# A decoder layer on one core: who issues the DMAs, in which order, and how often weights are loaded

## The chip, the cores and the metric

The kernel runs on one core of a Trainium2 chip. The core has a matrix engine (TensorE, PE in the profile; its weight loads are PEld), a vector engine (VectorE, DVE), an activation engine (ScalarE, ACT), a general engine (GpSimd, POOL) and SyncE (SP), which in this kernel issues DMAs. Every engine runs its own list of instructions in the order in which it was built and waits on semaphores. The metric is the time of one launch on the device in microseconds, lower is better.

## The reference, cut to what matters

Sixteen independent sequences of 256 positions and width 512 go through one layer of three parts, each followed by a residual sum and a layernorm (cut; biases and masks shortened):

```python
# 1: state-space mixer, 1024 channels (d), 16 states (n)
hs, gate = W_in_states @ x, W_in_gates @ x
hs   = silu(causal_conv4(hs))
dt   = softplus(W_dtproj @ (W_dt @ hs) + b)        # [d, l]
Bm, Cm = W_b @ hs, W_c @ hs                          # [n, l]
s    = exp(A * dt) * s + dt * Bm * hs                # scan over l, for each d, n
y    = (sum_n s * Cm + D * hs) * silu(gate)
x    = layernorm(x + W_out @ y)
# 2: cross attention, 16 heads of 16; x is read as [256 channels, 512 positions]
q, k, v = Wq @ x, Wk @ ctx, Wv @ ctx
x    = layernorm(x + softmax(mask * (q.k / 4) ...) @ v)
# 3: feed-forward, ternary weights, 8-bit activations
h    = silu(a) * b   with  a, b = quant(x) @ quant(w_gate_up)
x    = layernorm(x + quant(h) @ quant(w_down))
```

## The kernel before

Each batch (sequence) passes through stages that are cut into small closures ("thunks"). The table `WIN` gives each stage a window in time measured in batches: `P` and `R` (`prep`: input projection with convolution; time step, B and C, softplus), `M` (the scan, 34 thunks), `T` and `U` (gate and output projection of the two channel halves), `K`, `L` (keys, first layernorm, queries), `A` (values and attention, 10 steps of 4 parts), `N` (normalising the attention), `F` (feed-forward) and `W` (quantising weights, once). `place` spreads a stage's thunks over its window, and all thunks are called in the order of these times. So up to four batches are in work at once. The order of the calls is only a priority: the tile framework schedules the instructions itself, each engine's list included, with SyncE's list of DMAs among them, and puts in the semaphore waits.

Tiles come from pools by tag, each tag with a fixed number of buffers; a new tile waits until the oldest buffer of its tag is free. The parts that the change touches:

- **Weights.** `wload` (line 91) loads a tile with tag `wout`, 3 buffers, from SyncE's queue at the place of use. `project` (line 260) loads a `win` tile and uses it at once; `outproj` (line 502) loads four `wout` tiles for each of two row tiles `lt`, so each twice; `up` and `down` (lines 667 and 707) load the 8-bit tiles `fw` for each of two row tiles `t`.
- **Softplus** (line 321) makes dt and dt*u for eight channel tiles and stores them to a DRAM tile `dtd` (line 360). Its work tiles `e` and `l` share the tag `h` (8 buffers) with the scan.
- **Scan.** `fetch(d)` (line 373) reads `dtr` and `dur` back, replicated over the partitions, 512 KB each, one per channel tile. `unit(d, g)` (line 398) multiplies on POOL (line 403), makes four exps on ACT (line 409) and runs two scans on DVE (line 411). `tail`, two units later (`LAG`), multiplies by C on POOL (line 383); after four of them TensorE sums over the states (line 389).
- **Attention.** `split_store` (line 450) writes queries and keys as a high and a low part to `sq` and `sk` in DRAM (line 459). `fetch(g)` (line 519) reads two heads back into `qk` tiles (10 buffers). `step(i, c)` computes scores of head pair `i` for their maxima (lines 530 and 558) and, for pair `i - 2`, exps (line 564) and the products with the values (line 574). `maxima` (line 535) turns the maxima into two rows per head: it writes them to a DRAM tile `md` (line 547) and reads that into rows 62 to 65 of the query tile (line 548). The products go to `so` in DRAM (line 596). `norm` (line 603) reads sums and products back.

Every DMA of this kernel is issued by SyncE.

Of the kernel before, what the change touches and what calls it, by code (L numbers as in the profile page):

```python
# [13 lines left out]
ALU = mybir.AluOpType  # L14
# [22 lines left out]
WIN = {'P': (-1.15, -0.888), 'R': (-0.611, -0.455), 'M': (0.0, 0.8), 'T': (0.476, 0.576), 'U': (0.812, 0.912), 'L': (0.991, 1.041), 'K': (0.773, 0.826), 'A': (1.018, 1.938), 'N': (2.099, 2.147), 'F': (2.57, 3.237), 'W': (0.0, 1.0)}  # L37
# [5 lines left out]
HB = 8  # L43
PTB = 3
QKB = 10
F4B = 3
LAG = 2
# [4 lines left out]
def decoder_kernel(ctx, tc, x, xT, ctx_in, mask, winT, wdtT, wbcT, wdpT, woutT, dvec, wqkvT, bqk, bv, wguT, wdnT, out):  # L52
# [35 lines left out]
    def f4(shape, dt=F32):  # L88
        return ap_.tile(shape, dt, tag="f4", name=nm("f4"), bufs=F4B)

    def wload(src):
        w = mp.tile(list(src.shape), F32, tag="wout", name=nm("wout"), bufs=3)
        nc.sync.dma_start(out=w, in_=src)
        return w
# [21 lines left out]
    al = mt("h", [P, NDT, NB4, NS], HB)  # L116
# [36 lines left out]
    wq = const([P, 2, 256], F32, "wq")  # L153
# [3 lines left out]
    def setup_mask():  # L157
        nc.sync.dma_start(out=wq, in_=wqkvT[:, :, 0:256])
# [38 lines left out]
    def w_load(j):  # L197
        c, r = divmod(j, 2)
        src = wguT[:, 2 * r : 2 * r + 2, c * 512 : (c + 1) * 512] if c < 8 else wdnT[:, (c - 8) * 4 + 2 * r : (c - 8) * 4 + 2 * r + 2, :]
        w = mt("h", [P, 2, 512], HB)  # L200
        nc.sync.dma_start(out=w, in_=src)
        return w

    def setup_w():
# [4 lines left out]
        def total():  # L209
# [4 lines left out]
            ones = mt("h", [P, P], HB)  # L214
# [6 lines left out]
        def quant(j):  # L221
# [5 lines left out]
            q = at("fw", [P, 2, 512], 3, FP8)  # L227
# [32 lines left out]
    def project(ps_t, xt, c0):  # L260

        for i in range(2):
            w = mt("win", [P, 4, P], 3)
            nc.sync.dma_start(out=w, in_=winT[:, :, c0 + i * P : c0 + (i + 1) * P])
            for k in range(4):
                nc.tensor.matmul(ps_t[:, i, :], w[:, k, :], xt[:, k, :], start=k == 0, stop=k == 3)  # L266


    def prep(b):
        st = S[b]  # L270
        th = []

        def load():
            st["xT"] = xload(b)
            st["u"] = [None, None]

        def inproj(d0):
            hs = mm_ps([P, 2, L], "P")
            z = mt("tmp", [P, 2, L], 2)
            project(hs, st["xT"], d0 * P)  # L280
# [14 lines left out]
        def ts_bc():  # L295
            p = mm_ps([P, 512], "P")
            for d in range(NDT):
                if d % 4 == 0:
                    wdt = wload(wdtT[:, d : d + 4, :])
                nc.tensor.matmul(p[:, :L], wdt[:, d % 4, :], st["u"][d // 4][:, d % 4, :], start=d == 0, stop=d == NDT - 1)  # L300
            ts = mt("ts", [P, L], 1)
            nc.scalar.copy(ts, p[:, :L])
            st["ts"] = ts
            wbc = wload(wbcT)
            p2 = mm_ps([P, 512], "P")
            for d in range(NDT):
                nc.tensor.matmul(p2[:32, :L], wbc[:, d, :], st["u"][d // 4][:, d % 4, :], start=d == 0, stop=d == NDT - 1)
            bc = mt("tmp", [32, L], 2)
            nc.scalar.copy(bc, p2[:32, :L])
            bcd = dr.tile([32, L], F32, tag="bcd", name=nm("bcd"), bufs=2)  # L310
            nc.sync.dma_start(out=bcd, in_=bc)
            st["bcd"] = bcd
# [8 lines left out]
        def softplus():  # L321

            st["dtd"] = dr.tile([2, NDT, DB, NB4, L], F32, tag="dtd", name=nm("dtd"), bufs=3)
            xs, es, ls = [], [], []
            for hf in range(2):
                X = mt("dt", [P, 4, L], 2)
                xs.append(X)
                wdp = wload(wdpT[:, hf * 512 : (hf + 1) * 512])
                for i2 in range(2):
                    p = mm_ps([P, 2, L], "P")  # L330
                    for i in range(2):
                        c = (2 * i2 + i) * P
                        nc.tensor.matmul(p[:, i, :], wdp[:, c : c + P], st["ts"], start=True, stop=True)
                    for i in range(2):
                        d = hf * 4 + 2 * i2 + i
                        nc.scalar.activation(X[:, 2 * i2 + i, :], p[:, i, :], AF.Identity, bias=dv[:, d, 6:7])
                e = mt("h", [P, 4, L], HB)
                es.append(e)
                nc.scalar.activation(e, X, AF.Abs)
                nc.scalar.activation(e, e, AF.Exp, scale=-1.0)  # L340
            for hf in range(2):
                l = mt("h", [P, 4, L], HB)
                ls.append(l)
                nc.scalar.activation(l, es[hf], AF.Ln, bias=1.0)
            for hf in range(2):
                for i2 in range(2):
                    s = slice(2 * i2, 2 * i2 + 2)
                    X, e, l = xs[hf][:, s, :], es[hf][:, s, :], ls[hf][:, s, :]
                    t = mm_ps([P, 2, L], "P")
                    nc.scalar.activation(t, e, AF.Identity, bias=1.0)  # L350
                    nc.vector.scalar_tensor_tensor(t, t, 1.0, e, ALU.subtract, ALU.subtract)
                    nc.vector.scalar_tensor_tensor(t, X, 0.0, t, ALU.max, ALU.subtract)
                    nc.vector.tensor_tensor(t, t, l, ALU.add)
                    dtu = mt("dtu", [P, 2, L], 2)
                    nc.vector.tensor_tensor(dtu, t, st["u"][hf][:, s, :], ALU.mult)
                    nc.scalar.copy(X, t)  # L356
                    for k, src in ((0, X), (1, dtu)):
                        for i in range(2):
                            dst = st["dtd"][k, 4 * hf + 2 * i2 + i].rearrange("c g l -> g c l")
                            nc.sync.dma_start(out=dst, in_=src[:, i, :])  # L360

        th = [load] + [lambda d=d: inproj(d) for d in range(0, NDT, 2)]
        return {"P": th, "R": [ts_bc, bcast, softplus]}
# [3 lines left out]
    def scan(b):  # L367
        st = S[b]
        th = []
# [3 lines left out]
        def fetch(d):  # L373
            st["rep"] = []
            for k, tag in ((0, "dtr"), (1, "dur")):
                t = mt(tag, [P, NB4, L], 2)
                src = st["dtd"][k, d].rearrange("c g l -> c (g l)")
                nc.sync.dma_start(out=t, in_=src[None].broadcast_to([NB4, DB, NB4 * L]))
                st["rep"].append(t)
# [18 lines left out]
        def unit(d, g):  # L398
            if g == 0:
                fetch(d)  # L400
            dt, dtu = st["rep"]
            hh = mt("h", [P, NS // NB4, L], HB)
            nc.gpsimd.tensor_tensor(hh, st["B"], dtu[:, g, None, :].broadcast_to([P, NS // NB4, L]), ALU.mult)  # L403
            for h2 in range(2):
                t = dA_t[dA_i[0] % 2]
                dA_i[0] += 1
                for i in range(2):
                    j = 2 * h2 + i
                    nc.scalar.activation(t[:, i, 1:], dt[:, g, 1:], AF.Exp, scale=A[:, d, g, j : j + 1])  # L409
# [6 lines left out]
        for d in range(NDT):  # L416
            for g in range(NB4):
                th.append(lambda d=d, g=g: unit(d, g))
        th += [lambda: tail(pend.pop(0))] * LAG
        return th  # L420


    def attn(b):
        st = S[b]
        st["sq"], st["sk"] = sq_t[b % 2], sk_t[b % 2]
        th = []

        def load():
# [11 lines left out]
            mr = at("mr", [P, 64], 1)  # L440
            nc.sync.dma_start(out=mr, in_=mask[b, 0].rearrange("(a e) -> a e", a=8)[None].broadcast_to([16, 8, 64]))
            st["mr"] = mr
# [8 lines left out]
        def split_store(m, p, bcol, dst, slots_hi, slots_lo):  # L451
# [5 lines left out]
            for t, slots in ((hi, slots_hi), (lo, slots_lo)):  # L457
                for s in slots:
                    nc.sync.dma_start(
                        out=dst[m * 8 : m * 8 + 8, R0 + s * HD : R0 + (s + 1) * HD, :],  # L460
                        in_=t.bitcast(F32),
                    )

        def kproj():
            wk = wload(wqkvT[:, :, 256:512])
            for m in range(2):
                p = mm_ps([P, 512], "K")
                for k in range(2):
                    nc.tensor.matmul(p, wk[:, k, m * P : (m + 1) * P], st["ctx"][k], start=k == 0, stop=k == 1)
                split_store(m, p, 1, st["sk"], (0, 2), (1,))  # L470

        def vproj():
            wv = wload(wqkvT[:, :, 512:768])
            bvh = bv_t.rearrange("p (h d) -> p h d", h=NH)
            for s in range(0, 4, 2):
                p = mm_ps([P, 2, 256], "V")
                for i in range(2):
                    for k in range(2):
                        nc.tensor.matmul(p[:, i, :], st["ctx"][k][:, (s + i) * P : (s + i + 1) * P], wv[:, k, :], start=k == 0, stop=k == 1)
                for i in range(2):  # L480
                    v = vaug[:, s + i, :, 0:HD]
                    nc.vector.tensor_tensor(v, p[:, i, :].rearrange("p (h d) -> p h d", h=NH), bvh, ALU.add)
                    nc.scalar.mul(v, v, st["ms"][:, s + i : s + i + 1])

        def gate_load():
            st["xTg"] = xload(b)

        def gated(d0):
            g = mm_ps([P, 2, L], "G")
            project(g, st["xTg"], DI + d0 * P)  # L490
# [10 lines left out]

        def outproj(hf, lt):
            p = mm_ps([P, 512], "O")
            for i in range(4):
                w = wload(woutT[:, 4 * hf + i, :])
# [310 lines left out]
```

## Time and profile before

| | |
|---|---|
| median of 3 runs | 5132.09 us (5129.36 to 5134.6) |
| profiled execution | 5123.51 us |
| its span, first to last instruction | 5121.4 us |
| mean granted TensorE clock | 0.751 |
| busy: PE, DVE, POOL, ACT | 3462.3, 2966.0, 2544.8, 2421.9 us |
| DMA | 688.54 MB, mean 134 GB/s, 43.4% of 16 engines' time |
| first and last store of `out` | 1128.8 and 5117.1 us |

A profile is one execution. "Busy" is the time in which an engine has an instruction in work. The chain that ended last is followed back from the last instruction, at each step to what released it. A wait is named by the engine and line that waited and by what ended the wait. "SPq" is SyncE's instruction list itself, where DMAs are issued. The granted clock is the share of full clock that TensorE got.

### The profile page before, as it was taken

What the parts mean: (1) busy time and instruction counts of PE and PEld (TensorE: products, weight loads), DVE (VectorE), ACT (ScalarE), POOL (GpSimd) and SP (SyncE); (2) the same over time, 40 slices, a digit from 0 to 9 for tenths busy, and PEclk for the clock granted to TensorE, in tenths of its full rate; (3) what the DMA queues carried; (4) which work ended last, traced back from release to release, by engine and by line L of the source; (5) the groups of instructions that cost most, each with busy time, mean ns of one, the idle gap of its engine ahead of it and who ended that gap; (6) DMA issues with size and microseconds to landing.
All of it is one profiled execution on the core that took longest, in us unless ns stands there. A gap on an engine that the chain in (4) does not pass through costs nothing.

```text
span 5121.4 us, 50817 instructions
## 1 busy us (share of the span) xinstructions
PE 3462.3 (68%) x16386; PEld 1616.7 (32%) x16386; DVE 2966.0 (58%) x4254; ACT 2421.9 (47%) x4700; POOL 2544.8 (50%) x1367
## 2 busy tenths in 40 slices
PE   3234677867767777666768576686666768675876
PEld 2112333333323333322323223232332324332332
DVE  2566557565656666465556565465565655665543
ACT  2343446454454555435454454455445444544433
POOL 1645457465554555455445565355554544666100
PEclk7666676877777787777868778686776868777868
DMA  5455343544435453443534435344443534434233
GB/s 153 138 175 170 103 138 119 154 135 131 147 121 177 120 155 124 138 135 115 161 120 141 128 116 156 112 146 126 137 141 111 168 116 136 145 126 151 85 103 103
DMA packets 488723, 688.54 MB, mean 134 GB/s; under 512 B 53944, under 2 KB 266936, under 8 KB 488456
## 3 DMA queue, kind: packets, MB, share of 16 engines
q1 hardware_dynamic: 488456, 685.29, 43.4%
q8 instruction: 130, 2.13, 0.2%
q14 instruction: 137, 1.12, 0.1%
HBM read 569.15 MB, written 122.29 MB: 135 GB/s over the span
## 4 chain that ended last, share of the span: by engine, by line
PE 31%; DMA 27%; DVE 18%; ACT 9%; SPq 4%; issue 4%; POOL 1%; DVEq 0%; ACTq 0%; POOLq 0%
DVE h L411 9%; DMA wout<-in_woutT 8%; PE mm L266 6%; PE sc L530 6%; PE mm L389 4%; DVE mx L558 4%; PE mm L506 4%; DMA md<-mhl 3%; PE av L574 3%; DMA sq<-qf 3%; ACT pT L564 2%; DMA qk<-sk 2%; PE sc L718 2%; DMA fw<-dn_q 2%; ACT dA L409 2%
## 5 line engine op out<-in xcount | busy, mean ns | idle before, releaser
L403 POOL TENSOR_TENSOR h<-B,dur 128x1024 f32<-128x1024 f32 x512 | 1196.2, 2364 | 1272.4 <-PE mm L389 858.1
L383 POOL TENSOR_TENSOR h<-h,C 128x1024 f32<-128x1024 f32 x512 | 1199.3, 2363 | 371.0 <-DVE h L411 327.5
L409 ACT ACTIVATE dA<-dtr,A 128x255 f32<-128x255 f32 x2048 | 951.5, 473 | 855.7 <-DVE h L411 775.6
L530 PE MATMUL sc<-qk,qk 64*128 64x512 f32 x2048 | 926.9, 627 | 547.1 <-DMA qk<-sk 187.1
L411 DVE TENSOR_TENSOR_SCAN h<-dA,h 128x512 f32<-128x512 f32 x1024 | 1210.4, 1207 | 58.7 <-ACT dA L409 42.8
L558 DVE TENSOR_REDUCE mx<-sc 128x1 f32<-128x512 f32 x1024 | 673.5, 679 | 542.3 <-PE sc L530 539.2
L564 ACT ACTIVATE pT<-sc 128x512 f32<-128x512 f32 x1024 | 582.2, 592 | 773.4 <-PE sc L530 768.8
L530 PEld LDWEIGHTS sc<-qk,qk 64*128 64x128 f32 x2048 | 363.0, 232 | 1229.4 <-issue 626.5
L266 PE MATMUL mm<-xT,win 128*128 128x256 f32 x2048 | 559.2, 428 | 161.4 <-DMA win<-in_winT 69.0
L506 PE MATMUL mm<-wout,u 128*128 128x512 f32 x512 | 329.3, 752 | 418.2 <-DMA wout<-in_woutT 392.6
L266 PEld LDWEIGHTS mm<-xT,win 128*128 128x128 f32 x2048 | 426.9, 215 | 287.7 <-ACT dt L356 60.5
L574 PE MATMUL av<-pT,vaug 128*32 128x256 f32 x4096 | 436.4, 495 | 49.6 <-ACT pT L564 47.4
L389 PE MATMUL mm<-h,sel 128*32 128x256 f32 x4096 | 397.3, 472 | 94.6 <-POOL h L383 86.7
L286 DVE SCALAR_TENSOR_TENSOR tmp<-mm,cw,tmp 128x255 f32<-128x255 f32 (+2 forms) x384 | 182.7, 478 | 247.0 <-ACT tmp L283 240.7
L507 DVE TENSOR_TENSOR xres<-mm,xres 128x512 f32<-128x512 f32 x64 | 43.8, 686 | 401.0 <-PE mm L506 398.5
L506 PEld LDWEIGHTS mm<-wout,u 128*128 128x128 f32 x512 | 99.2, 225 | 515.4 <-DMA wout<-in_woutT 360.5
L389 PEld LDWEIGHTS mm<-h,sel 128*32 128x32 f32 x4096 | 151.9, 131 | 306.5 <-issue 170.3
L718 PE MATMUL sc<-fw,f 128*128 128x512 fp8e4 x512 | 137.4, 415 | 140.9 <-DMA fw<-dn_q 140.6
L245 POOL TENSOR_SCALAR lrs<-lmv 128x2 f32<-128x2 f32 x48 | 10.0, 218 | 392.0 <-DVE lmv L243 390.9
L621 POOL TENSOR_TENSOR qk<-qk,qk 128x512 f32<-128x512 f32 x32 | 40.6, 1269 | 329.1 <-DMA qk<-sr 126.5
L574 PEld LDWEIGHTS av<-pT,vaug 128*32 128x32 f32 x4096 | 97.7, 122 | 275.0 <-ACT pT L564 131.5
L678 PE MATMUL sc<-fw,xqT 128*128 128x512 fp8e4 x512 | 164.9, 454 | 23.3 <-DVE mx L558 13.4
(116 smaller groups left out, 3373.7 us busy)
## 6 DMA issues: line engine op xcount, KB each, us to landing
win<-in_winT SPq DMA_DIRECT2D x256, 256.0 KB
dtr<-dtd SPq DMA_DIRECT2D x128, 512.0 KB
dur<-dtd SPq DMA_DIRECT2D x128, 512.0 KB
wout<-in_woutT SPq DMA_DIRECT2D x256, 256.0 KB
fw<-gu_q SPq DMA_DIRECT2D x256, 256.0 KB
qk<-sq SPq DMA_DIRECT2D x128, 256.0 KB
qk<-sk SPq DMA_DIRECT2D x128, 256.0 KB
fw<-dn_q SPq DMA_DIRECT2D x128, 256.0 KB
```

The costliest lines, as they stand in the source:

```text
L266: nc.tensor.matmul(ps_t[:, i, :], w[:, k, :], xt[:, k, :], start=k == 0, stop=k == 3)
L383: done.append((hh, nc.gpsimd.tensor_tensor(hh, hh, st["C"], ALU.mult)))
L389: m = nc.tensor.matmul(red[DB * g : DB * g + DB, :L], sel, h[:, j, :], start=j == 0, stop=j == NS // NB4 - 1, tile_position=(0, DB * g))
L403: nc.gpsimd.tensor_tensor(hh, st["B"], dtu[:, g, None, :].broadcast_to([P, NS // NB4, L]), ALU.mult)
L409: nc.scalar.activation(t[:, i, 1:], dt[:, g, 1:], AF.Exp, scale=A[:, d, g, j : j + 1])
L411: nc.vector.tensor_tensor_scan(seg, t.rearrange("p n l -> p (n l)"), seg, 0.0, ALU.mult, ALU.add)
L506: nc.tensor.matmul(p, st["u"][hf][:, i, lt * P : (lt + 1) * P], w, start=i == 0, stop=i == 3)
L530: nc.tensor.matmul(p, lhs[rows, c * P : (c + 1) * P].bitcast(F32R), rhs[rows, :].bitcast(F32R), start=True, stop=True)
L558: nc.vector.tensor_reduce(st[("mx", i)][:, j, c : c + 1], p, AX.X, ALU.max)
L564: x = nc.scalar.activation(e[:, j, :], p, AF.Exp, scale=DSC)
L574: m = nc.tensor.matmul(av[32 * k : 32 * k + 32, :], vaug_f[:, c, c0 : c0 + 32], e[:, j, t * L : (t + 1) * L], start=c == 0, stop=c == 3, t ...
L718: nc.tensor.matmul(p, hT[:, 4 * q + i, :], w[:, i, :], start=q + i == 0, stop=q == 3 and i == 3)
```

## The change

All thunks now go into one heap with a time each (`at_time`), and a thunk can put a later one there (`defer`). SyncE's list is taken from the framework's scheduler: its DMAs stand in the order in which the thunks issue them. The other engines' lists are still scheduled. With it:

- every load has a thunk of its own, most of them `LEAD` = 0.08 of a batch ahead of the use; `wout` and `fw` tiles are loaded once and used for both row tiles, with four buffers each, and `win` has four; other weights have tag `wr`, 3 buffers;
- stores of `so`, of the high parts of queries and keys, of dt and of B and C are issued by ScalarE; stores that stay with SyncE are mostly deferred by 0.01 to 0.03;
- `maxima` writes its rows with four DMAs from SBUF to SBUF, without `md`;
- softplus is cut into its two halves, has work tiles `s` (3 buffers) of its own, and writes dt*u over `e`; `dtr` and `dur` are fetched in halves of 256 KB;
- `norm` is cut into four thunks, and the product of its reciprocal sums with the mask moves from DVE to POOL;
- buffers: `h` 7 instead of 8, `pT` 2 instead of 3, `qk` 8 instead of 10; `LAG` 1 instead of 2;
- the times of all stages are new; the scan takes the whole batch time instead of 0.8 of it.

The diff, cut to its core:

```diff
-HB = 8
-PTB = 3
-QKB = 10
-F4B = 3
-LAG = 2
+HB = 7
+PTB = 2
+QKB = 8
+LEAD = 0.08
+LAG = 1
...
+    heap = []
+    now = [0.0]
+    def at_time(t, f):
+        uid[0] += 1
+        heapq.heappush(heap, (t, uid[0], f))
+    def defer(dt, f):
+        at_time(now[0] + dt, f)
+    def wload(src, tag="wr", bufs=3, dt=F32):
+        w = mp.tile(list(src.shape), dt, tag=tag, name=nm(tag), bufs=bufs)
         nc.sync.dma_start(out=w, in_=src)
         return w
...
+    def win_load(c0):
+        return [wload(winT[:, :, c0 + i * P : c0 + (i + 1) * P], "win", 4) for i in range(2)]
...
+            nc.scalar.dma_start(out=st["bcd"], in_=bc)
...
+        def softplus(hf):
+            Xf = mt("s", [P, 4, L], 3)
+            ef = mt("s", [P, 4, L], 3)
...
+                nc.scalar.activation(X, e, AF.Ln, bias=1.0)
+                nc.vector.tensor_tensor(t, t, X, ALU.add)
+                nc.vector.tensor_tensor(e, t, st["u"][hf][:, s, :], ALU.mult)
+                nc.scalar.copy(X, t)
+                for i in range(2):
+                    nc.scalar.dma_start(out=dst(0, d + i), in_=X[:, i, :])
+            for d in range(4):
+                nc.sync.dma_start(out=dst(1, 4 * hf + d), in_=ef[:, d, :])
...
+        for t, f in (
+            (-0.5 - LEAD, ts_load), (-0.5, time_step), (-0.46 - LEAD, bc_load), (-0.46, bc), (-0.3, bcast),
+            (-0.38 - LEAD, lambda: dt_load(0)), (-0.38, lambda: softplus(0)),
+            (-0.26 - LEAD, lambda: dt_load(1)), (-0.26, lambda: softplus(1)),
+        ):
+            at_time(b + t, f)
...
-        def fetch(d):
+        def fetch(d, g):
             for k, tag in ((0, "dtr"), (1, "dur")):
+                t = mt(tag, [P, 2, L], 2)
+                src = st["dtd"][k, d, :, g : g + 2, :].rearrange("c g l -> c (g l)")
...
+                t = b + (4 * d + g + 0.5) / 32
+                if g % 2 == 0:
+                    at_time(t - 0.05, lambda d=d, g=g: fetch(d, g))
+                at_time(t, lambda d=d, g=g: unit(d, g))
...
+            store(nc.scalar, hi, slots_hi)
+            defer(0.01, lambda: store(nc.sync, lo, slots_lo))
...
+        def wout_load(hf):
+            st[("wout", hf)] = [wload(woutT[:, 4 * hf + i, :], "wout", 4) for i in range(4)]
         def outproj(hf, lt):
             for i in range(4):
-                w = wload(woutT[:, 4 * hf + i, :])
-                nc.tensor.matmul(p, st["u"][hf][:, i, lt * P : (lt + 1) * P], w, start=i == 0, stop=i == 3)
+                nc.tensor.matmul(p, st["u"][hf][:, i, lt * P : (lt + 1) * P], st[("wout", hf)][i], start=i == 0, stop=i == 3)
...
-            md = dr.tile([G, 2, 4, P], F32, tag="md", name=nm("md"), bufs=4)
-            for j in range(G):
-                nc.sync.dma_start(out=md[j].rearrange("q a t -> a q t"), in_=mhl[4 * j : 4 * j + 4].bitcast(F32))
-            nc.sync.dma_start(out=QS[KROWS - 2 : KROWS + 2], in_=md.rearrange("j q a t -> (j q) (a t)"))
+            def store():
+                for j in range(G):
+                    for q in range(2):
+                        r = KROWS - 2 + 2 * j + q
+                        nc.sync.dma_start(out=QS[r : r + 1, :], in_=mhl[4 * j : 4 * j + 4, q, :].bitcast(F32))
+            defer(0.03, store)
...
-                        nc.sync.dma_start(out=dst.rearrange("h r t -> (h r) t"), in_=o[64 * t : 64 * t + 64, :])
+                        nc.scalar.dma_start(out=dst.rearrange("h r t -> (h r) t"), in_=o[64 * t : 64 * t + 64, :])
...
-            nc.vector.tensor_tensor(rc, rc, st["mr"], ALU.mult)
+            nc.gpsimd.tensor_tensor(rc, rc, st["mr"], ALU.mult)
...
+        for hf, t in ((0, 0.56), (1, 1.03)):
+            for i in range(2):
+                at_time(b + t + 0.06 * i - LEAD, lambda d=4 * hf + 2 * i: gate_load(d))
+                at_time(b + t + 0.06 * i, lambda d=4 * hf + 2 * i: gated(d))
+                at_time(b + t + 0.12 + 0.06 * i, lambda hf=hf, i=i: outproj(hf, i))
+            at_time(b + t + 0.1 - LEAD, lambda hf=hf: wout_load(hf))
+        for t, f in (
+            (1.27, ln1), (1.28 - LEAD, lambda: w_qkv(0)), (1.28, lambda: qproj(0)), (1.3, lambda: qproj(1)),
+            (1.38 - LEAD, lambda: w_qkv(2)), (1.38, lambda: vproj(0)), (1.4, lambda: vproj(2)), (1.36, lambda: fetch(0)),
+            (2.42, norm_sums), (2.48, norm_scale), (2.52, norm_load), (2.58, norm),
+        ):
+            at_time(b + t, f)
+        for i in range(NH // G + S2):
+            for c in range(4):
+                at_time(b + 1.42 + 0.096 * i + 0.024 * c, lambda i=i, c=c: step(i, c))
...
+            st[("wu", c)] = [wload(gu_q[4 * k + c].rearrange("p (a b) -> p a b", a=4), "fw", 4, FP8) for k in range(2)]
...
+            st["wd"] = [wload(dn_q[q].rearrange("p (a b) -> p a b", a=4), "fw", 4, FP8) for q in range(4)]
...
-    for _, f in sorted(seq, key=lambda e: e[0]):
-        f()
+    with tc.manual_schedule(engines={mybir.EngineType.SP}):
+        while heap:
+            now[0], _, f = heapq.heappop(heap)
+            f()
```

## The prediction

> **What bounds the kernel now.** I read the page's header and its chain first, to see whether one engine or the waits set the time.
>
> ```profile
> PE 3462.3 (68%) x16386; PEld 1616.7 (32%) x16386; DVE 2966.0 (58%) x4254; ACT 2421.9 (47%) x4700; POOL 2544.8 (50%) x1367
> ...
> PE 31%; DMA 27%; DVE 18%; ACT 9%; SPq 4%; issue 4%; POOL 1%; DVEq 0%; ACTq 0%; POOLq 0%
> ```
>
> No engine is full: TensorE, the busiest, works 68% of 5121.4 us. The chain that ended last spends 27% (1383 us) in DMA and 4% (205 us) in SyncE's queue, so transfers that come late are the largest cause that is not arithmetic. Next I took the waits of all engines, and then SyncE's own, to see which transfers are late and why.
>
> ```profile
> PE mm L506 <- DMA wout<-in_woutT: 392.6, 56, 24.5
> ...
> PE sc L530 <- DMA qk<-sk: 187.1, 17, 20.1
> ...
> PE sc L718 <- DMA fw<-dn_q: 140.6, 19, 17.1
> ...
> PE mm L266 <- DMA win<-in_winT: 69.0, 11, 17.1
> ...
> PE sc L530 <- DMA qk<-md: 59.0, 9, 11.4
> ```
> ```profile
> SPq L548 <- DMA md<-mhl: 386.6, 96, 11.3
> SPq L264 <- PE mm L266: 271.2, 110, 12.2
> SPq L547 <- DVE mhl L542: 199.5, 64, 10.1
> SPq L675 <- PE sc L678: 191.7, 68, 9.4
> SPq L93 <- PE mm L506: 174.9, 137, 3.3
> ```
>
> Columns: total us, times, longest. TensorE idles 1635.9 us; the rows that a DMA ends add up to 872 us of it (the five above are 848.3). SyncE, the only DMA issuer, stands in line for others: 386.6 us for the DRAM hop of the maxima, and 638 us for TensorE to release weight buffers. Whatever is queued behind such a wait is late too. The third view is one stall, in the timeline and as a window:
>
> ```profile
> 2672.04 5.59 SPq L93 DMA_DIRECT2D wout<-in_woutT  x2
> ...
> 2687.30 2.08 PE L506 MATMUL mm<-wout,u 128*128 128x512 f32 x2 [23.36 <-DMA wout<-in_woutT]
> ```
> ```profile
> 2600.00:2620.00 20.00, 19.01 (x116) 9.93 (x114) 9.41 (x16) 13.28 (x27) 7.27 (x13) 0.93 0.42 133
> ...
> 2660.00:2687.00 27.00, 3.94 (x17) 1.69 (x14) 0.97 (x2) 2.31 (x7) 0.54 (x1) 0.52 0.41 135
> ```
>
> In the window's row, after its length, stand busy us of PE, PEld, DVE, ACT and POOL, then the granted clock. TensorE's order puts the output projection first, its weights were issued only at 2672, behind a run of dtd stores, and for 27 us all engines together do almost nothing. In steady state a batch takes about 310 us (stores of `out` from the fifth to the ninth lie 309 to 312 us apart); such a stall in each is 8% of it.
>
> **The change part by part.** The sum is made against the profiled execution: 5123.51 us, span 5121.4, so 2.1 us lie outside it. It stands 8.6 us (0.2%) under the median 5132.09; I add that back at the end.
>
> *Weights ahead and once.* 128 loads of wout, 128 of gu_q and 64 of dn_q go (320 x 256 KB, 84 of 688.5 MB). At a DMA share of 43% the bytes are no bound and earn nothing; the earlier issue does. wout is put 0.10 of a period before use (31 us of 310), the others 0.08 (25 us), longer than the longest wait above. In the order of the built kernels SyncE's DMAs that wait on TensorE fall from 1100 to 243. Of wout's 392.6, dn_q's 140.6 and gu_q's 12.4 us of TensorE's waits I take 85%: 464 us; of win's 69.0 half, since its fourth buffer comes free only 3 us ahead in two places: 35 us. Next in line after the weights is the scan's own chain, which is why I do not take all.
>
> *First queries and keys.* Query projection to first fetch gets 0.06 to 0.08 of a period (19 to 25 us), where the row shows waits up to 20.1. Half of 187.1: 94 us.
>
> *Maxima rows inside SBUF.* Three DMAs per group with a landing between become four without; 128 more issues at 0.26 to 0.29 us are 35 us of SyncE, hidden by its idle time. The wait of 386.6 us leaves SyncE's queue. Its direct worth is the 59.0 us of TensorE's waits for md; I take 41. The rows of 512 values go to one partition each, a shape that the trace lacks: its nearest row, md to qk with 8 KB, issues in 0.26 us. Consumers come a whole step (30 us) later, so even 10 us of landing hides; if not, 128 groups by 10 us is the upper bound, 1280 us. I take 0.
>
> Gains: 464 + 35 + 94 + 41 = 634 us.
>
> *Stores on ScalarE.* 528 DMAs move to an engine that computes: 256 so, 128 dtd, 128 sq and sk, 16 bcd.
>
> ```profile
> L360 SPq DMA_DIRECT2D dtd<-dt x128: 503/598/4818, 83.9 to 4498.7; - x128
> ...
> L596 SPq DMA_DIRECT2D so<-qf x256: 451/550/6012, 556.3 to 5029.6; - x128
> ```
>
> By the medians (ns, the middle value) this is 256 x 0.55 + 128 x 0.60 + 128 x 0.63 + 16 x 0.37 = 304 us; with the long ones summed from the trace's records, 439 us. On SyncE nothing but DMAs stood behind them. On ScalarE behind them stand the exps of the scan (DVE's scan waits for these, then POOL) and of the scores (TensorE's `av` matmuls wait). ScalarE goes from 47% to 56% busy. The Trainium skill, "DMA: Bandwidth & Descriptors", section "Issuing engines are not separate DMA queues", speaks against the move: DMAs of all issuers share the same 16 engines, and another issuer only saves the sequencer's time. By the rule the transfers gain nothing, and 439 us is a plain debit on a computing engine; the row says how much of that engine's time is on the path: its share of the chain, 9% over 47% busy, makes a fifth, 84 us. Between 84 and 439 I take 146, a third, as a late exp holds two engines.
>
> *A wait added with it.* In the built kernel all DMAs take eight completion semaphores in turn, and each waits until the DMA eight places before it has landed, whoever issued that one; 442 of the 528 carry this wait. Lower bound 0 (landed by then); upper: all pay what SyncE paid in the nearest row (L93 waiting for wout: 89.8 us in 35, so 2.6 us), 1149 us. SyncE has 2554 such waits and few showed, so I take one in four, 287 us, half on the path: 144 us.
>
> *Program order on SyncE.* The four dtu stores at the end of each softplus now hold the queue until DVE is done, with dtr and dur fetches behind them that lead by only 0.05 (15.5 us). Before, one batch's softplus ran from 2611 to about 2651, 20 us a half: 4.5 us short, twice in 16 batches, 144 us at most for POOL and ACT, who wait for the fetch. POOL is idle half the time; I take a quarter, 36 us, and keep 0 and 144. The halved fetches add 256 issues (0.57 us, 146 us of SyncE), hidden: SyncE issues 1938 of 5121 us.
>
> *Small ones.* 18 more activation-table loads of 1283 ns: 23 us. The product of the sums (0.90 us, 16 times) moves to POOL: idle there, 0. Fewer buffers (PTB 2, QKB 8; HB 7, but softplus and the weight setup leave that pool): 0, as `av` follows its exps at once; at worst one exp pair (1.2 us) for each of 512 steps, 614 us.
>
> *Clock.* In the busiest window above the granted clock is 0.93, in the stall 0.52. The Trainium skill, "TensorE: Matmul & The Clock Gate", section "The HAM clock gate", has two states, half clock after an idle window of about 3.4 us and full after a busy one. By the rule, with every idle window gone 3462 us at 0.751 become 2600, 862 us less; by the rows, removing a sixth of the idle time lifts the mean to perhaps 0.77, 90 us of busy time. Part lies under other waits; I take 60.
>
> Sum: 634 - 146 - 144 - 36 - 23 + 60 = 345. 5123.5 - 345 = 4778, plus 8.6 = 4787. I expect some gain more from the windows in which all engines stand still, where one late transfer delays independent streams too (the 386.6 us of SyncE's wait earned only 41 above); a tenth of it: **4750 us**, 7.4% faster.
>
> **Rivals.**
>
> *ScalarE's queue takes it all (slower).* Place: lines 369, 474 and 617 of the changed kernel, in front of the exps. If all 442 waits cost 2.6 us and the issues 439, ScalarE holds 1588 us more (78% busy); half on the path is 794, and with the remaining terms as before: 5132 - (634 + 60 - 794 - 36 - 23) = 5291 us. It decides from 635 us on the path, 1.2 us per DMA. For it: `dtd` issues of 4.8 us and the coupling of both queues. Against: at 8 DMAs back most have landed in the trace.
>
> *The streams' own latency takes the place.* DMA waits vanish, but POOL still waits for TensorE (858.1 us at line 403) and the exps for DVE's scan (775.6). Then only the 8% stall of wout halves or less: about 5050 us, up to 5170 with the debits of ScalarE. For it: 18% of the chain is DVE. Against: in the stall all five idle, which is loss for every stream.
>
> *TensorE becomes the bound.* All 872 us go and the clock rises to 0.85: 3462 x 0.751 / 0.85 = 3059 busy plus the 764 us of other waits plus half of the debits (175) and prologue and drain of some 300 in which it lacks work: about 4300 us.
>
> *The change doesn't do what it says:* loads placed earlier still queue behind blocked ones, since SyncE's order is now fixed. It shows as wout's wait unchanged; the time stays with 5130 or rises by the debits.
>
> **How the numbers follow.** Forecast 0.50 (4450 to 5000 its own range), TensorE-bound 0.09, latency 0.11 (half of it faster), ScalarE's queue 0.26, order unchanged 0.04. A measurement tells this kernel from no change at about 0.2%. Faster 0.50 + 0.09 + 0.05 = 0.64; same 0.02; slower 0.34. For eight in ten the range reaches from 4330 (below it the TensorE-bound half) to 5360 (ScalarE's queue above its middle).
>
> **What would show it.** Right: `PE <- DMA wout` below 60 us in total, no maxima wait on SyncE, DMA's share of the chain under 15%, granted clock at least 0.77, batches about 285 us apart. ScalarE: its queue on the chain under 5%, waits of its stores under 300 us. Wrong: a large ScalarE-queue share, or exps whose idle time a DMA ends; waits of POOL and ACT for dtr and dur above 150 us; 310 us or more between batches.

## The result, and the profile after

The changed kernel takes 5734.8 us (median of 4 runs, 5728.48 to 5739.34) against 5133.35 us: the ratio is 1.1169, with a 95% interval of 1.115 to 1.1189. It is 11.7% slower where 7.4% faster was forecast, and lies above the range of 4330 to 5360. The profiled execution has a span of 5726.7 us and a mean granted clock of 0.734.

The page's header and chain, as in the first fence of the prediction:

```profile
PE 3643.7 (64%) x16386; PEld 1733.0 (30%) x16386; DVE 2959.9 (52%) x4238; ACT 2422.8 (42%) x4750; POOL 2553.4 (45%) x1383
...
DMA 40%; PE 19%; DVE 16%; SPq 7%; ACT 7%; POOL 6%; issue 5%; ACTq 0%; DVEq 0%; POOLq 0%
DMA dur<-dtd 18%; DVE h L427 8%; DMA win<-in_winT 6%; POOL h L419 5%; PE sc L547 4%; DMA dtr<-dtd 4%; DMA dtd<-s 4%; PE mm L273 4%; DVE mx L579 3%; DMA s<-in_wguT 2%; PE av L595 2%; SPq L396 2%; ACT dA L425 2%; SPq L101 2%; PE mm L407 2%
```

DVE, ACT and POOL do the same work as before, within 12 us each. DMA's share of the chain went up from 27% to 40% and SyncE's queue from 4% to 7%, although 81 MB less is moved (607.48 MB). And the transfer at the head of the chain is not a weight: it is `dur`, which the scan reads back, with 18% of the span. The waits of all engines, and then SyncE's own (line numbers are those of the changed kernel: 419 is POOL's first product of the scan, 425 the exps, 396 the scan's fetches, 101 the loads of weights, 540 the fetch of queries and keys, 474 the stores of their parts, 567 the maxima rows, 371 the stores of dt*u):

```profile
POOL h L419 <- DMA dur<-dtd: 2166.0, 212, 131.6
DVE h L427 <- POOL h L419: 868.2, 174, 16.4
ACT dA L425 <- DMA dtr<-dtd: 856.5, 169, 14.4
...
PE mm L273 <- DMA win<-in_winT: 253.8, 47, 20.5
```
```profile
SPq L540 <- PE sc L547: 454.3, 49, 20.0
SPq L474 <- DVE qf L471: 443.0, 47, 34.4
SPq L540 <- PE sc L556: 422.2, 22, 35.0
SPq L567 <- ACT mhl L558: 342.0, 48, 27.0
SPq L371 <- DVE s L366: 329.4, 32, 31.2
```

Before, `dur` held POOL for 107.3 us, nearly all of it in one wait:

```profile
POOL h L403 <- DMA dur<-dtd: 107.3, 2, 105.9
```

Now it does so 212 times at 256 fetches, about 10 us each. The prediction had named waits of POOL and ACT for `dtr` and `dur` above 150 us as a sign of being wrong; they are 3022 us. wout, the largest DMA wait of TensorE before with 392.6 us, has left the list. The five largest of SyncE's rows are all DMAs of other stages that wait for their producer or their buffer. One such stop in SyncE's timeline, its row among SyncE's waits, and what POOL does meanwhile:

```profile
2715.36 0.78 SPq L331 DMA_DIRECT2D C<-bcd  x1
2735.87 0.32 SPq L540 DMA_DIRECT2D qk<-sq  x1
2736.23 0.43 SPq L540 DMA_DIRECT2D qk<-sk  x1
2736.76 4.11 SPq L567 DMA_DIRECT2D qk<-mhl  x4
2740.92 0.56 SPq L396 DMA_DIRECT2D dtr<-dtd  x1
2741.58 0.54 SPq L396 DMA_DIRECT2D dur<-dtd  x1
```
```profile
SPq L540 <- PE sc L556: 20.0, 1, 20.0
```
```profile
2729.89 2.36 POOL L401 TENSOR_TENSOR h<-h,C 128x1024 f32<-128x1024 f32 x1 [0.90 <-DVE h L427]
2750.67 4.66 POOL L419 TENSOR_TENSOR h<-B,dur 128x1024 f32<-128x1024 f32 x2 [18.42 <-DMA dur<-dtd]
```

SyncE issues nothing for 20 us, because the next DMA of its list, the query fetch, waits for a `qk` buffer. Six DMAs stand between it and `dur`. POOL runs out of work at 2732.25 us, `dur` is issued at 2741.58, and POOL goes on 9 us later. The batches now lie 326 to 338 us apart in the steady part instead of about 310.

### The profile page after: what moved, and what is told of

It is laid out like the page before. It is cut to its first block, busy times and chain, and to the rows that moved or that the text cites. A ratio compares the mean times of both kernels' runs of the same rounds, so it can differ in the third digit from the quotient of the medians.

```text
span 5726.7 us, 50523 instructions
## 1 busy us (share of the span) xinstructions
PE 3643.7 (64%) x16386; PEld 1733.0 (30%) x16386; DVE 2959.9 (52%) x4238; ACT 2422.8 (42%) x4750; POOL 2553.4 (45%) x1383
## 2 busy tenths in 40 slices
DMA packets 480510, 607.48 MB, mean 106 GB/s; under 512 B 50600, under 2 KB 267432, under 8 KB 480248
## 4 chain that ended last, share of the span: by engine, by line
DMA 40%; PE 19%; DVE 16%; SPq 7%; ACT 7%; POOL 6%; issue 5%; ACTq 0%; DVEq 0%; POOLq 0%
DMA dur<-dtd 18%; DVE h L427 8%; DMA win<-in_winT 6%; POOL h L419 5%; PE sc L547 4%; DMA dtr<-dtd 4%; DMA dtd<-s 4%; PE mm L273 4%; DVE mx L579 3%; DMA s<-in_wguT 2%; PE av L595 2%; SPq L396 2%; ACT dA L425 2%; SPq L101 2%; PE mm L407 2%
## 5 line engine op out<-in xcount | busy, mean ns | idle before, releaser
L425 ACT ACTIVATE dA<-dtr,A 128x255 f32<-128x255 f32 x2048 | 923.9, 470 | 1678.1 <-DMA dtr<-dtd 856.5
L547 PE MATMUL sc<-qk,qk 64*128 64x512 f32 x2048 | 972.1, 615 | 656.4 <-DVE mx L579 244.6
L273 PE MATMUL mm<-xT,win 128*128 128x256 f32 x2048 | 621.9, 462 | 529.4 <-DMA win<-in_winT 253.8
L547 PEld LDWEIGHTS sc<-qk,qk 64*128 64x128 f32 x2048 | 379.9, 226 | 1339.2 <-DVE mx L579 408.6
L273 PEld LDWEIGHTS mm<-xT,win 128*128 128x128 f32 x2048 | 463.0, 235 | 665.2 <-issue 274.8
L407 PEld LDWEIGHTS mm<-h,sel 128*32 128x32 f32 x4096 | 151.9, 129 | 392.6 <-issue 190.3
L524 PE MATMUL mm<-wout,u 128*128 128x512 f32 x512 | 241.7, 621 | 19.1 <-issue 9.7
L347 PE MATMUL mm<-ts,wr 128*128 128x256 f32 x256 | 112.7, 589 | 206.9 <-DMA wr<-in_wdpT 121.4
L715 DVE SCALAR_TENSOR_TENSOR hq<-hq,sc 128x512 f32<-128x512 f32 x128 | 87.5, 683 | 265.4 <-ACT hq L714 265.2
L712 PE MATMUL sc<-fw,xqT 128*128 128x512 fp8e4 x512 | 190.5, 511 | 17.4 <-DVE mx L579 16.6
L718 PE MATMUL sc<-fw,xqT 128*128 128x512 fp8e4 x512 | 173.2, 472 | 22.4 <-ACT pT L585 21.0
L313 PE MATMUL mm<-u,wr 128*128 128x256 f32 x256 | 96.5, 556 | 71.8 <-DMA wr<-in_wdtT 51.4
```

What stands on the lines that cost most here:

```text
L273: nc.tensor.matmul(ps_t[:, i, :], ws[i][:, k, :], xt[:, k, :], start=k == 0, stop=k == 3)
L407: m = nc.tensor.matmul(red[DB * g : DB * g + DB, :L], sel, h[:, j, :], start=j == 0, stop=j == NS // NB4 - 1, tile_position=(0, DB * g))
L425: nc.scalar.activation(t[:, i, 1:], dt[:, 1:], AF.Exp, scale=A[:, d, g, j : j + 1])
L524: nc.tensor.matmul(p, st["u"][hf][:, i, lt * P : (lt + 1) * P], st[("wout", hf)][i], start=i == 0, stop=i == 3)
L547: nc.tensor.matmul(p, lhs[rows, c * P : (c + 1) * P].bitcast(F32R), rhs[rows, :].bitcast(F32R), start=True, stop=True)
L712: nc.tensor.matmul(pa, st["xqT"][:, k, t * P : (t + 1) * P], wa[:, k, :], start=k == 0, stop=k == 3)
```

## The experiments

All are changes of the kernel after, unless said otherwise. Two more theories stood beside the prediction's own rivals once the profile was seen: that the *fixed order* of SyncE's list lets late producers hold the scan's fetches, or that the fetches are late by themselves, because halved tiles leave them *too little lead and buffer*. The third is the rival of the forecast, the *stores on ScalarE*.

**SyncE's list given back to the scheduler.**

```diff
-    with tc.manual_schedule(engines={mybir.EngineType.SP}):
-        while heap:
+    while heap:
```

> The changed kernel with one part undone: SyncE's DMAs are again ordered by the framework's scheduler, all else (early loads, ScalarE's stores, halved fetches, buffers, times) as changed. Theory (SyncE's fixed order lets late producers hold the scan's fetches): POOL's waits for dur fall from 2166 us to under 500, time 4750 to 5150. Rival 1 (lead and buffers of the halved fetch too small, whatever stands before it): waits for dur above 1500, time 5550 or more. Rival 2 (stores on ScalarE): exps stay late, time 5550 or more.

Measured: 4738.27 us, ratio to before 0.9241 (0.9224 to 0.9257). One line undone takes 997 us off and turns 11.7% slower into 7.6% faster. Leads, buffers, halved fetches and ScalarE's stores are still those of the change. Its waits:

```profile
POOL h L419 <- PE mm L407: 553.7, 42, 28.6
...
POOL h L419 <- DMA dur<-dtd: 377.9, 75, 104.0
```

POOL's largest wait is now for TensorE's sums over the states; `dur` falls from 2166 to 377.9 us, 104 of them one wait. So the loss needs the fixed order. The scheduler lists the computing engines anew as well, though: matched by line and tile, half of TensorE's 16386 matmuls stand 96 or more places from where the changed kernel has them. How much of the 997 us comes through these lists, this run alone does not say. The sum of SyncE's own waits does not tell the kernels apart (its rows sum to 3190 us here, 3282 in the kernel before, 3835 in the changed kernel); what is listed behind a wait must count for more.

**Single blockers moved.** First the query and key fetch alone, two quarter steps later:

```diff
-            if c == 0 and i + 1 < NH // G:
+            if c == 2 and i + 1 < NH // G:
                 fetch(i + 1)
```

Then, in a second kernel, this and three kinds of stores deferred further: the low parts, the maxima rows and the four dt*u stores of softplus (the last by 0.06, cut here):

```diff
-            defer(0.01, lambda: store(nc.sync, lo, slots_lo))
+            defer(0.04, lambda: store(nc.sync, lo, slots_lo))
...
-            defer(0.03, store)
+            defer(0.06, store)
```

> The changed kernel with the fetch of the next query and key tiles placed two quarter steps later, when their buffers have been free for 16 us. Theory (fixed order; this fetch is the largest blocker with 876 us of SyncE's waits): that wait falls under 200 us, part of it passes to the next blocker, time 5450 to 5650. Rival 1 and 2: within 1% of 5735.

> As the previous one, and also the stores of the low parts, of the maxima rows and of dt*u stand 9 to 20 us later in SyncE's order; nothing moves to another queue. Theory: SyncE's waits for DVE, ACT and PE fall from about 2200 us to under 700, POOL's for dur under 900, time 4900 to 5300. Rival 1: waits for dur stay above 1500, time above 5500. Rival 2: time above 5500.

Measured: 5670.98 us (1.1046, 1.1023 to 1.107) and 5672.84 us (1.1056, 1.1039 to 1.1073). The first is 1.1% faster than the changed kernel, just above the range expected and just outside the 1% of the rivals; POOL's waits for `dur` did not fall (2228.5 us). The second was expected at 4900 to 5300 and brought nothing more. Its SyncE waits, and POOL's for `dur`:

```profile
SPq L571 <- ACT mhl L562: 891.8, 57, 34.7
SPq L373 <- DVE s L366: 286.2, 23, 28.5
SPq L478 <- DVE qf L475: 285.9, 31, 25.4
```
```profile
POOL h L423 <- DMA dur<-dtd: 2085.3, 208, 125.2
```

The stop at the query fetch is gone from the large rows, and the maxima store took it over: 342 us became 721.6 in the first run and 891.8 in the second, where it is deferred twice as far. Taking away one stop lets SyncE run on to the next one.

**More lead for the fetches, with a third buffer.**

```diff
-HB = 7
+HB = 6
-                t = mt(tag, [P, 2, L], 2)
+                t = mt(tag, [P, 2, L], 3)
-                    at_time(t - 0.05, lambda d=d, g=g: fetch(d, g))
+                    at_time(t - 0.085, lambda d=d, g=g: fetch(d, g))
```

> The changed kernel with SyncE's fixed order kept, the scan's fetches placed 0.085 instead of 0.05 of a batch ahead, with a third buffer each and the h buffers cut from 7 to 6 to make room. POOL's 212 waits for dur are 10.2 us each. If SyncE stands at a fixed place relative to the slowest stream (the attention), 11 us more of lead take most of these away: waits under 700 us, time 4900 to 5250. If SyncE's stops are longer than any lead (a stop of one stream simply stops all), waits stay above 1400 and the time above 5450; a POOL wait for h buffers would be the price of the sixth.

Measured: 5775.77 us (1.1252, 1.1232 to 1.1273).

```profile
POOL h L419 <- DMA dur<-dtd: 2071.0, 200, 131.9
```

A 70% longer lead takes 4% off these waits. Lead in this list is a place behind other DMAs, not a time. The rival of too little lead falls with this run and with the next, where the shorter lead and two buffers are enough. The kernel is 0.7% slower than the changed one; whether the missing `h` buffer does that was not tested.

**The fetches taken out of the list:** `dtr` to ScalarE, `dur` to GpSimd.

```diff
-                nc.sync.dma_start(out=t, in_=...)
+                (nc.scalar, nc.gpsimd)[k].dma_start(out=t, in_=...)
```

> The changed kernel with only the scan's fetches taken out of SyncE's list: dtr is issued by ScalarE, dur by GpSimd, with the same lead, buffers and sizes. Theory: the fetches no longer queue behind blocked DMAs; waits for dur and dtr fall from 3022 us in sum to under 800, time 4900 to 5250, less what 256 issues cost GpSimd ([...]hidden as it is 45% busy). Rival 1 (lead and buffers): waits stay above 2000, time within 3% of 5735. Rival 2: no gain.

Measured: 5003.3 us (0.9757, 0.974 to 0.9774), faster than before, with SyncE's order still fixed. POOL's and ACT's waits:

```profile
POOL h L419 <- DMA dur<-dtd: 61.9, 41, 6.4
...
ACT dA L425 <- DMA dtr<-dtd: 173.6, 17, 17.1
```

3022 us of waits become 235.5, and 732 of the 997 us come back, with TensorE's list nearly that of the changed kernel (matched as above, half of its matmuls stand within 2 places). The lists of ScalarE and GpSimd, in which the fetches now stand, are made by the scheduler, so that a list of their own and a list ordered by the scheduler are not told apart here. The other 265 us are what is left of the fixed order, together with what differs in the computing engines' lists; waits for `win` (164.9 us) and `xT` (119.0) are still on TensorE here and nearly absent in the scheduler's run (5.8 and 18.8).

**The attention taken out instead.** A theory after the deferring run was that the attention's DMAs set the pace of the list.

```diff
-                nc.sync.dma_start(out=t_, in_=st[src][2 * g : 2 * g + 2]...)
+                nc.gpsimd.dma_start(out=t_, in_=st[src][2 * g : 2 * g + 2]...)
-                        nc.sync.dma_start(out=QS[r : r + 1, :], ...)
+                        nc.scalar.dma_start(out=QS[r : r + 1, :], ...)
```

> The changed kernel with SyncE's fixed order, its lead and its buffers, and the scan's fetches left on SyncE; instead the attention's DMAs leave it: the query and key tiles are fetched by GpSimd, the maxima rows are stored by ScalarE. Deferring these DMAs (5673 us) and a longer lead (5776 us) had not helped, so the theory now is that in one fixed list each DMA of the attention, whichever stands next, paces the scan's fetches behind it: taking the attention out frees the scan as taking the scan out did (5003 us). Expected 4950 to 5300 and POOL's waits for dur under 1000 us. If the scan's fetches are late for a reason of their own (landing time, dt*u stores before them), the time stays above 5500.

Measured: 5700.92 us (1.1111, 1.107 to 1.1151), waits for `dur` 2000 us. The theory was wrong: with the attention's fetches and maxima rows gone, SyncE stops elsewhere:

```profile
SPq L371 <- DVE s L366: 772.0, 44, 35.8
SPq L101 <- PE sc L712: 443.0, 23, 35.1
SPq L474 <- DMA qk<-mhl: 412.5, 21, 31.6
SPq L474 <- DVE qf L471: 345.3, 40, 35.1
```

**Only loads left in the list.** On top of the last edit, all stores of the batches that were still on SyncE, and the reads of sums and products, go to GpSimd (`nc.sync.dma_start` becomes `nc.gpsimd.dma_start` at lines 236, 371, 628, 634, 640, 641, 763 and for the low parts at 474).

> The changed kernel with SyncE's fixed order, lead and buffers, and a list that holds only loads of weights and inputs, the scan's fetches and B and C: every other DMA of the batches (all stores of results, the attention's fetches, the reads of sums and products) is issued by GpSimd or ScalarE, whose lists the scheduler orders. The run before it (attention taken out, 5701 us) showed the stops passing on to the dt*u and key stores that were left. If SyncE's stops behind late producers are the cause, whichever they are, none is left here: waits for dur under 900 us and 4850 to 5150, GpSimd paying some 40 DMAs per batch. If waits for dur stay above 1500 us and the time above 5500, the scan's fetches are late in a fixed list even without stops by stores: by waits for free buffers, or by their own place.

Measured: 5315.36 us (1.0368, 1.0342 to 1.0394), waits for `dur` 993 us: between the two expectations. The claim that no stop would be left was wrong:

```profile
SPq L101 <- PE sc L712: 1133.0, 64, 38.4
SPq L396 <- ACT dA L425: 466.9, 93, 13.0
```

A load that waits for a free buffer stops the list like a store: loads of line 101 wait for the feed-forward's matmuls (line 712), which free the `fw` tiles, for 1133 us, and the scan's fetches themselves wait 466.9 us for the exps that free theirs. Taking out the stores and the attention's reads together brings 420 us, net of what GpSimd pays for issuing them: its busy time is 2914.5 us instead of 2553.4.

**ScalarE's stores given back, under the scheduler's order** (`bcd`, `dtd`, `so` and the high parts of queries and keys).

```diff
-nc.scalar.dma_start(...)
-            store(nc.scalar, hi, slots_hi)
+nc.sync.dma_start(...)
+            store(nc.sync, hi, slots_hi)
```

> The version with the scheduler's order on SyncE (4738 us), and all 528 stores of ScalarE given back to SyncE. The prediction's debit for ScalarE (146 us of issue and 144 us of waits on the path) says 4440 to 4600 here. If the stores on ScalarE cost nothing on the path, the time stays within 1% of 4738; if they help, because SyncE's queue is the scarcer one, it rises above 4790.

Measured: 4707.57 us (0.9174, 0.9149 to 0.9199), 31 us or 0.7% less than with ScalarE's stores (the two intervals lie just apart). So they do cost, but a ninth of the 290 us that the prediction had put on the path. In the fixed order they were not tried.

**No early placing, under the scheduler's order.**

```diff
-LEAD = 0.08
+LEAD = 0.002
```

> The scheduler's order with the loads of weights and inputs called at their use instead of 0.08 of a batch ahead; the scan's fetches keep 0.05. By the prediction's account the early placing is most of the gain (464 of 634 us): 5000 to 5150. If the scheduler places loads by itself, so that the call's time hardly matters: within 1.5% of 4738, and the gain comes from loading once and the stages' new times.

Measured: 4724.25 us (0.921, 0.9181 to 0.9238), the same as 4738 within the intervals. Under the scheduler it hardly matters when a load is called; TensorE's rows show no wait for wout here either. Whether this lead counts where the order is fixed was not tried.

**Two parts of the change alone, on the kernel before.** wout loaded once, at its use:

```diff
             for i in range(4):
                 w = wload(woutT[:, 4 * hf + i, :])
+                for t in range(2):
+                    nc.tensor.matmul(ps2[t], st["u"][hf][:, i, t * P : (t + 1) * P], w, ...)
```

> The kernel before with only wout loaded once for both row tiles, still at the place of use; both accumulators take the two PSUM banks of their tag. The prediction's account (PE's wait of 392.6 us is mostly the lateness of the load, not the number of loads) says half of it goes: 4900 to 5060. If only the early placing matters: within 1% of 5132. If the bank pair blocks the scan's sums: above 5180.

Measured: 5105.35 us (0.994, 0.9922 to 0.9958). TensorE's wait for wout goes only from 392.6 to 350.7 us with half the loads, and the gain is 0.6%:

```profile
PE mm L509 <- DMA wout<-in_woutT: 350.7, 28, 25.5
```

```diff
-            md = dr.tile([G, 2, 4, P], F32, tag="md", name=nm("md"), bufs=4)
...
+            for j in range(G):
+                for q in range(2):
+                    nc.sync.dma_start(out=QS[r : r + 1, :], in_=mhl[4 * j : 4 * j + 4, q, :].bitcast(F32))
```

> The kernel before with only the maxima rows written straight from SBUF to SBUF, four DMAs without a landing between. SyncE loses 386.6 us of waits, PE at least 59 us. Prediction's direct worth: 41 us, 5090; if a standing SyncE delays all streams, 4900 to 5050; if the one-partition writes land late, above 5132.

Measured: 5083.6 us (0.9896, 0.9879 to 0.9913): 1.0% or 52 us, close to the 41 that the prediction had, and short of what a standing SyncE was thought to be worth.

**The fastest version.** Scheduler's order, stores on SyncE, and the scan's fetches on ScalarE and GpSimd.

> The fastest version so far (4708 us: the scheduler's order, all stores on SyncE) with the scan's fetches issued by ScalarE and GpSimd, which held SyncE for some 550 us by waiting for free dtr and dur buffers. If these waits delay other loads: 4550 to 4680. If not: 4680 to 4760, GpSimd losing about 200 us of its idle time; above 4760 if dtr's issue in ScalarE's list delays exps.

Measured: 4689.85 us (0.9145, 0.9116 to 0.9175). It is 8.5% faster than the kernel before and 18% faster than the changed one. Against 4708 us the intervals overlap, so the last edit is not shown to help.

In one view, POOL's waits for `dur` against the time:

| SyncE's list | POOL waits for dur, us | time, us |
|---|---|---|
| fixed (the change) | 2166 | 5735 |
| fixed, fetches longer ahead | 2071 | 5776 |
| fixed, query fetch later | 2228 | 5671 |
| fixed, stores deferred | 2085 | 5673 |
| fixed, attention out | 2000 | 5701 |
| fixed, only loads | 993 | 5315 |
| fixed, fetches out | 62 | 5003 |
| scheduler's | 378 | 4738 |
| scheduler's, no lead | 335 | 4724 |
| scheduler's, stores on SyncE | 462 | 4708 |
| scheduler's, stores on SyncE, fetches out | 39 | 4690 |
| scheduler's, kernel before | 107 | 5133 |

In the fixed order the time falls roughly with these waits; between fixed and scheduled runs other waits count too.

## Why the prediction was wrong

**The step that failed is "Program order on SyncE", taken at 36 us with a bound of 144.** It had the mechanism: a DMA that waits in a fixed list delays the scan's fetches behind it. It named one kind of stop, the dt*u stores, and took 4.5 us for each, the part of 20 us of softplus that exceeds the lead. The runs showed 997 us. Four things were missed. The five largest rows of SyncE's waits are stops of four kinds, not one, and 876 us of them are the query fetch, which waits for a buffer; "fewer buffers" (`qk` 8 instead of 10) had been put at 0. The named stop itself, the dt*u stores, took 329 us in 32 waits, 10 us each. The lead was subtracted from the stop as if both were counted on one clock; but the fetch is issued only after the stop, and the run with the longer lead showed that its nominal length hardly matters. And the price was summed by place: removing one kind or several (the query fetch, the deferred stores, the attention) brought at most 1.1%, since the next stop takes over.

**The bound was where the error could have been seen.** The prediction took the fall of SyncE's waits for TensorE from 1100 to 243 as a good sign. What was left was enough: the query fetch alone waits 876 us for TensorE, and the other three of the five largest rows wait 1114 us for DVE and ACT. The question to ask of the changed list is which DMA with the shortest need stands behind which with the latest producer. It is `dur`, needed about every 20 us, in one list with all the others.

**"Weights ahead and once", 464 us.** The predicted sign came: wout left the list of waits. But the early placing was not shown to do it: under the scheduler's order a lead of 0.002 gives the same time as 0.08, and wout's wait is absent there too. Loading wout once is worth 28 us alone and leaves most of its wait. In the fixed order `win`'s wait rose to 253.8 us, where half of 69.0 was to go.

**"Maxima rows", 41 us:** 52 us alone. The issue cost was too low: the one-partition rows issue in 602 ns (median), not 260 to 290, so 313 us of SyncE instead of 177 for the DRAM way. The gain of 52 us is net of that.

**"Stores on ScalarE" and "a wait added", 290 us on the path:** 31 us, under the scheduler's order. The rival that forecast a slower kernel was right in its sign and wrong in its place: in the changed kernel the waits of ScalarE that end with the landing of a store sum to at most 95 us, the largest row 18.4 us, and ScalarE's queue has 0% of the chain. Of the two ends for the issue time the lower (84 us) was nearer. The rule that the prediction took from the Trainium skill, "DMA: Bandwidth & Descriptors", section "Issuing engines are not separate DMA queues", is that another issuer saves only issue time. Here the measurement says more: the 512 fetches of the scan hold SyncE for 375 us of issue in the changed kernel, and with ScalarE and GpSimd issuing them the time fell by 732 us, because they no longer stood behind SyncE's stops.

**"Clock", 60 us:** with the stalls in the scan it went the other way, 0.734, and TensorE is busy 181 us longer for the same instructions. In the scheduler's version it rose to 0.779, and TensorE is busy 50 us less. Changed kernel, kernel before and scheduler's version have TensorE idle for 36, 32 and 28% of the span at 0.734, 0.751 and 0.779; the direction agrees with the Trainium skill, "TensorE: Matmul & The Clock Gate", section "The HAM clock gate", where idle windows lower the clock.

**The forecast number.** The scheduler's version, with every part of the change but the fixed order, takes 4738 us, and 4750 were forecast. This is no confirmation of the sum: its largest gain (early placing) measured nothing in the run without lead, and its largest debit (ScalarE) a ninth. wout once and the maxima in SBUF, measured alone on the kernel before, would make some 80 of the 394 us there. What the rest is (8-bit weights loaded once, softplus out of the scan's buffers, the stages' new times) was not separated and stays open. Open too is why single stops last 25 to 35 us; and the fixed order with the old times was not tried. One figure of a rival does not follow from its own terms: half of an 8% stall would be about 205 us and the time about 4930, where it has 5050.

## What to carry to other kernels

When a queue's order is fixed by hand, look for the consumer with the shortest period, and ask of each DMA ahead of its loads what it waits for, producers and free buffers alike; where streams of different pace shared the list here, the whole list ran at the pace of whatever was late at the moment. Try the short-period stream on another queue, or leave the order to the scheduler; repairing stops one by one brought at most 1.1% here. And a wait that left one queue is no gain until the list behind the remaining ones is read.

## What was not expected of the hardware

A 256 KB fetch of `dur` issued by GpSimd took 4.8/6.4/13.6 us (least, median, most) from issue to landing and 0.69 us of GpSimd's time to issue; on SyncE the issue took 0.55 us (median), and after the one shown above POOL went on 9 us later. The 256 of them on GpSimd added 174 us to its 2553 busy us; under the scheduler's order the kernel with them is no slower than the one without (4690 against 4708 us). One-partition rows of 2 KB cost about twice the issue time of the 4 KB writes to DRAM that they replaced (602 against 292 ns).
